# A mixture of experts whose product down is turned around: hidden units stationary, weights moving, and the shared expert as a ninth term of the same sum

## The chip, the cores and the metric

The kernel runs on one core of one Trainium2 chip, in f32 throughout. The metric is the time of one execution on the device, in microseconds. Engines are named as in the profile: PE is TensorE (PEld its weight loads), DVE is VectorE, ACT is ScalarE, POOL is GpSimd, SP is SyncE, which only issues DMAs here.

## The reference, cut to what matters

The input x has 8 batches of 1024 tokens with 128 features. Three layers follow one another, each behind a layer norm and each added to x: a feed-forward layer with weight 0.5, a causal attention with one head of 128, and the same feed-forward layer again. The feed-forward layer is a mixture of 16 experts with 64 hidden units each; a token uses its 4 best, and a shared expert with 64 hidden units is added for every token.

```python
scores = sigmoid(xt @ gate_w.T)
_, idx = top_k(scores + gate_b, 4)
w = take(scores, idx); w = w / w.sum() * 2.5
comb[t, idx] += w
...
for e in range(16):
    h = silu(xt @ gate_e.T) * (xt @ up_e.T)
    y = y + comb[:, e, None] * (h @ w2_e.T)
y = y + (silu(xt @ gate_s.T) * (xt @ up_s.T)) @ w2_s.T
x = x + 0.5 * y
```

## The kernel before

**Tiling.** All 16 experts are computed for all tokens, and comb is zero for those a token doesn't use. The unit of feed-forward work is a group of 512 tokens (W), four tiles of 128 (GT = 4). There are 8 batches x 2 groups x 2 feed-forward layers = 32 groups (NPER), done one after the other in a fixed order in which the second layer of one batch alternates with the first layer of the batch that is four further on. The 16 x 64 = 1024 hidden units are cut into NP = 8 blocks of 128, two experts each.

**One group.** The normed tokens lie transposed as hT, features by 512 tokens. For each block k, `up` (line 273) issues two matmuls of 128x512, gate (L271) and up (L284), with the weights stationary in the array; ScalarE takes silu of the one (L286), VectorE multiplies it with the other into hidT (L288), and `weigh` (L292, GpSimd) multiplies that by the token weights cb. Then `down` (L297) sums over the 8 blocks: the block of w2, wd, is stationary and hidT's 512 tokens move through it, so that y comes out transposed, features by tokens, in PSUM bank 0. `close` (L308, VectorE) adds the shared expert's part ys and leaves yT in SBUF. In the next group's time `add` has TensorE transpose yT in four pieces (L330), and VectorE adds half of it to x (L333); in the second layer a DMA stores it (L335). The last group does this in two halves (`add_last`, L318 to L321).

**The shared expert** is done for two groups at once (class Shared): `up` makes 128 columns of gate and up per group (L348), ScalarE and VectorE make h of it (L352, L353), with one group's 64 units on partitions 0 to 63 and the other's on 64 to 127. `down` multiplies the two halves by wsd on two row tiles of the array (L362, tile positions 0 and 64), and ScalarE copies the result to ys (L368).

**The route.** `turn` transposes the tokens (L174), route_a and route_b make the logits (L199, L208), top_a to top_c find the four best on VectorE and end with comb (L217 to L245), and `spread` transposes comb (L254), copies it, writes it to DRAM and reads it back broadcast over partitions as cb, all on SP's queue.

**Order.** Nothing is left to a scheduler. Every group's time p has 18 slots, U0 to U8 along its eight up steps and D0 to D8 along its eight down steps, and `at(p, slot, f)` puts work into a slot; its instructions go to each engine's queue in that order. Of group p's route, norm_a stands at (p-2, U5), norm_b at (p-2, D1), turn at (p-2, D4), route_a at D5, route_b and score at D7, top_a and top_b at D8, top_c at (p-1, U1) and spread at (p-1, U3). The attention's queries stand in between: a query's scores at U7, D2 or D4, its exp some slots later, its transpositions (L460, copied out at L464 by ScalarE or L466 by VectorE), and its product with v (L472, added to x at L476); those of one of the three queries fall on U3 of the next group. Shared.up stands at U0 and Shared.down at U2 of every second group; `add` of group p stands at (p+1, U3), and the statistics of the attention's norm for it at (p+1, U5) and (p+1, U7).

**PSUM.** There are eight banks of 128x512. Bank 0 holds y, banks 0 to 3 the up and gate products in turn, 2 to 5 the queries' scores, 4 and 5 also the shared expert. Everything else asks `other_bank`, which hands out the bank longest unused of 6, 7 and those of 1 to 5 that `hold` doesn't keep in this slot or a neighbouring one; banks 6 and 7 are handed out in any case. A bank that is still being read makes the next writer wait.

Of the kernel before, what the change touches and what calls it, by code (L numbers as in the profile page):

```python
# [9 lines left out]
F32 = mybir.dt.float32  # L10
AF = mybir.ActivationFunctionType
ALU = mybir.AluOpType
# [3 lines left out]
P = 128  # L16
# [10 lines left out]
def kernel(  # L27
# [14 lines left out]
    nc = tc.nc  # L42

    B, S, D = x.shape
    E = gate_w.shape[1]
    I = w_sh_down.shape[0]
    NT = S // P
    GT = 4
    NG = NT // GT
    W = GT * P  # L50
    EI = E * I
    NP = EI // P
# [3 lines left out]
    const = ctx.enter_context(tc.tile_pool(name="const", bufs=1))  # L56
# [3 lines left out]
    work = ctx.enter_context(tc.tile_pool(name="work", bufs=3))  # L60
# [8 lines left out]
    def bank(i, n=1):  # L69
        return psum[:, i * W : (i + n) * W]  # L70
# [5 lines left out]
    def other_bank():  # L76
        for n in by_age:
            free = not held[n] & {now[0] - 1, now[0], now[0] + 1} and now[0] >= 0
            if n > 5 or free:
                by_age.remove(n)  # L80
                by_age.append(n)
                return bank(n)

    def tiles_of(ap):
        return ap.rearrange("p (j q) -> p j q", q=P)

    ident = const.tile([P, P], F32, name="ident")
# [14 lines left out]
    xs, mvs = [None] * B, {}  # L102
# [27 lines left out]
    wd = const.tile([P, NP, D], F32, name="wd")  # L130
    nc.sync.dma_start(out=wd, in_=w_down.rearrange("(n p) d -> p n d", p=P))

    wsd = const.tile([P, D], F32, name="wsd")
    for n in range(2):
        nc.sync.dma_start(out=wsd[n * I : (n + 1) * I, :], in_=w_sh_down)
    wqkv = const.tile([P, 3, D], F32, name="wqkv")
    cs = const.tile([P, 2, S], F32, name="cs")

# [6 lines left out]
    def stats(key, b, tiles):  # L145

        if key not in mvs:
            mvs[key] = small.tile([P, NT, 2], F32, tag="mv", name=f"mv_{key}", bufs=16)
        for t in tiles:
            st = small.tile([P, 6], F32, tag="st", name=f"st_{key}_{t}")  # L150
            nc.vector.bn_stats(st, xs[b][:, t, :])
            nc.vector.bn_aggr(mvs[key][:, t, :], st)
# [26 lines left out]
    class Group:  # L179
# [111 lines left out]
            hid = self.hidT[:, k, :]  # L291
            nc.gpsimd.tensor_tensor(hid, hid, self.cb[:, k, :], ALU.mult)  # L292

        def down(self, k):
            if k == 0:
                self.y = bank(0)
            nc.tensor.matmul(  # L297
                self.y, wd[:, k, :], self.hidT[:, k, :], start=(k == 0), stop=(k == NP - 1)
            )

        def close(self):

            self.yT = work.tile([P, W], F32, tag="yT", name=f"yT_{self.nm}", bufs=2)
            halves = [slice(0, W)]
            if self.n == NPER - 1:
                halves = [slice(0, W // 2), slice(W // 2, W)]
            for c in halves:
                nc.vector.tensor_tensor(self.yT[:, c], self.y[:, c], self.ys[:, c], ALU.add)  # L308

        def add_last(self):  # L310

            H = GT // 2
            for n, queue in enumerate((nc.scalar, nc.sync)):
                yp = tiles_of(other_bank())[:, :H, :]
                t = self.g * GT + n * H
                for j in range(H):
                    k = n * H + j
                    nc.tensor.transpose(yp[:, j, :], self.yT[:, k * P : (k + 1) * P], ident)  # L318
                xg = xs[self.b][:, t : t + H, :]
                nc.vector.scalar_tensor_tensor(xg, yp, 0.5, xg, ALU.mult, ALU.add)  # L320
                queue.dma_start(  # L321
                    out=out[self.b].rearrange("(t p) d -> p t d", p=P)[:, t : t + H, :], in_=xg
                )

        def add(self):
            if self.n == NPER - 1:
                return self.add_last()
            yp = tiles_of(other_bank())
            for j in range(GT):
                nc.tensor.transpose(yp[:, j, :], self.yT[:, j * P : (j + 1) * P], ident)  # L330
            tiles = slice(self.g * GT, (self.g + 1) * GT)
            xg = xs[self.b][:, tiles, :]
            nc.vector.scalar_tensor_tensor(xg, yp, 0.5, xg, ALU.mult, ALU.add)  # L333
            if self.layer == 1:
                nc.sync.dma_start(  # L335
                    out=out[self.b].rearrange("(t p) d -> p t d", p=P)[:, tiles, :], in_=xg
                )

    class Shared:
# [5 lines left out]
        def up(self):  # L345
# [3 lines left out]
            for n, gr in enumerate(self.pair):  # L349
# [3 lines left out]
                nc.vector.tensor_tensor(  # L353
                    self.h[n * I : (n + 1) * I, :], s_ps[I:, :], ss[I:, :], ALU.mult
                )

        def down(self):
            H = W // 2
            for c in (slice(0, H), slice(H, W)):
                for n in range(2):  # L360
                    rows = slice(n * I, (n + 1) * I)
                    nc.tensor.matmul(  # L362
                        bank(5 - n)[:, c], wsd[rows, :], self.h[rows, c], start=True, stop=True,
                        tile_position=(n * I, 0),
                    )
            for n, gr in enumerate(self.pair):
                gr.ys = work.tile([P, W], F32, tag="ys", name=f"ys_{gr.nm}", bufs=2)
                nc.scalar.copy(gr.ys, bank(5 - n))  # L368

# [116 lines left out]
    NPER = NG * len(order)  # L488
# [7 lines left out]
    def at(p, slot, *fs):  # L496
        jobs.setdefault((p, slot), []).extend(fs)
# [3 lines left out]
    def when(p, slot):  # L501
        return p * len(slots) + slots.index(slot)

    def hold(banks, first, last):
        for n in banks:
            held[n] |= set(range(when(*first), when(*last) + 1))

    for p in range(NPER):
        hold((0,), (p, "U1"), (p, "D8"))
        hold((1,), (p, "U1"), (p, "U8"))  # L510
        hold((2, 3), (p, "U1"), (p, "D1"))
# [4 lines left out]
    queue = [(b, i) for b in range(B) for i in range(NT)]  # L516
# [47 lines left out]
    for p, gr in enumerate(groups):  # L564
        steps = (
            gr.norm_a, gr.norm_b, gr.turn, gr.route_a, gr.route_b, gr.score, gr.top_a, gr.top_b,
            gr.top_c, gr.spread,
        )
        if p == 1:
            steps = steps[1:]  # L570
            places = [(0, s) for s in ("U3", "U5", "U6", "U8", "D0", "D1", "D2", "D3", "D6")]
        else:
            places = [(p - 2, s) for s in ("U5", "D1", "D4", "D5", "D7", "D7", "D8", "D8")]
            places += [(p - 1, "U1"), (p - 1, "U3")]
        if p > 0:
            for f, place in zip(steps, places):
                at(*place, f)
        if gr.layer == 1:
            for t in range(gr.g * GT, (gr.g + 1) * GT):
                assert done[gr.b, t] < when(p - 2, "U5")  # L580

        if p % 2 == 0:
            pair = Shared(groups[p : p + 2])
            if p == 0:
                at(0, "D0", pair.up)
                at(0, "D3", pair.down)
                hold((4, 5), (0, "D0"), (0, "D4"))
            else:
                jobs[p, "U0"] = [pair.up] + jobs.get((p, "U0"), [])
                at(p, "U2", pair.down)  # L590
                hold((4, 5), (p, "U0"), (p, "U3"))

        at(p + 1, "U3", gr.add)
        if gr.layer == 0:
            t = gr.g * GT
            for s in ("U5", "U7"):
                at(p + 1, s, lambda b=gr.b, t=t: stats(f"a{b}", b, (t, t + 1)))
                t += 2


    for b in range(2, B):
        p = turn_of[0, b, 0]
# [13 lines left out]
    def run(p, slot):  # L616
        now[0] = when(p, slot)
        for f in jobs.pop((p, slot), []):
            f()

    gr = groups[0]
# [17 lines left out]
    for p, gr in enumerate(groups):  # L639
        run(p, "U0")  # L640
        for k in range(NP):
            gr.up(k)
            if p == 0 and k < 2:
                run(p, f"U{k + 1}")
                if k == 1:
                    gr.weigh(k)
            else:
                gr.weigh(k)
                run(p, f"U{k + 1}")
        for k in range(NP + 1):  # L650
            if k < NP:
                gr.down(k)
            if k == NP - 1:
                gr.close()
            run(p, f"D{k}")
    for p in (NPER, NPER + 1):
        for slot in slots:
# [73 lines left out]
```

## Time and profile before

| | |
|---|---|
| median of 3 runs | 994.64 us |
| lowest, highest | 994.27, 995.35 us |
| the profiled execution's own time | 994.21 us |
| its span in the profile | 992.3 us |
| TensorE's granted clock | 1.0 |
| product down (L297) | 512 matmuls, mean 599 ns |
| shared product down (L362) | 128 matmuls, mean 402 ns |
| transposition of y (L330) | 124 matmuls, mean 273 ns |
| ScalarE's copy to ys (L368) | 32, mean 589 ns |
| VectorE's sum yT (L308) and its addition to x (L333) | 33 at 673 ns and 31 at 681 ns |

The profile gives an instruction's line, engine, operation and tiles. A matmul of f32 appears as two records, a transposition as one, each with a load of its own on PEld. Matmuls are pipelined, so the records overlap and their mean duration is longer than the distance from one to the next. "Idle before" is the time in which an engine did nothing ahead of an instruction, with the releaser that ended it. The chain that ended last is followed back from the last instruction through what released each.

### The profile page before, as it was taken

How to read it: one execution, taken by the hardware profiler on the slowest of the kernel's cores; microseconds unless marked ns; L12 is line 12 of the kernel's file. 1: busy time of each engine (PE TensorE's matmuls, PEld its weight loads, DVE VectorE, ACT ScalarE, POOL GpSimd, SP SyncE). 2: the span in 40 equal slices, each digit the busy share in tenths (PEclk: the TensorE clock that was granted, in tenths of full speed). 3: DMA queues.
4: the chain of work that ended last, by engine and by line, in shares of the span. 5: the costliest groups of instructions: out<-in, count | busy, mean ns of one | idle time of the engine just before them, and what ended most of it. 6: DMA issues, size and time to landing. Idle time of an engine off the chain costs nothing.

```text
span 992.3 us, 11654 instructions
## 1 busy us (share of the span) xinstructions
PE 979.5 (99%) x3654; PEld 516.8 (52%) x3654; DVE 671.5 (68%) x2035; ACT 442.2 (45%) x798; POOL 450.5 (45%) x379
## 2 busy tenths in 40 slices
PE   8999999999999999999999999999999999999998
PEld 5444455555555555555555555555555555455543
DVE  5776787668666677766768756776667756665543
ACT  3444545444544445443544444544444444443331
POOL 2455556145633463344625455333643455423444
PEclk9999999999999999999999999999999999999999
DMA  6655443043413532145303453044421344134440
GB/s 165 163 118 105 87 87 87 2 107 87 87 28 70 119 86 48 40 97 118 87 18 70 97 118 81 8 84 97 98 59 42 73 97 94 33 68 97 97 97 21
DMA packets 56909, 80.25 MB, mean 81 GB/s; under 512 B 3600, under 2 KB 23440, under 8 KB 56720
## 3 DMA queue, kind: packets, MB, share of 16 engines
q1 hardware_dynamic: 55568, 78.26, 35.4%
q10 hardware_dynamic: 1280, 1.26, 0.4%
q8 instruction: 28, 0.46, 0.2%
q14 instruction: 33, 0.27, 0.1%
HBM read 74.27 MB, written 5.24 MB: 80 GB/s over the span
## 4 chain that ended last, share of the span: by engine, by line
PE 93%; DVE 3%; ACT 1%; DMA 1%; issue 0%; POOL 0%; SPq 0%; POOLq 0%; DVEq 0%
PE psum L297 22%; PE psum L271 21%; PE psum L284 21%; PE psum L472 6%; PE psum L433 6%; PE psum L460 3%; PE psum L348 3%; PE psum L400 3%; PE psum L174 2%; PE psum L362 2%; PE psum L414 1%; PE psum L199 1%; PE psum L330 1%; DMA cb<-cd 1%; PE psum L254 1%; PE psum L141 1%
## 5 line engine op out<-in xcount | busy, mean ns | idle before, releaser
L292 POOL TENSOR_TENSOR hidT<-hidT,cb 128x512 f32<-128x512 f32 x256 | 323.0, 1269 | 502.5 <-DVE hidT L288 464.4
L271 PE MATMUL psum<-hT,wg 128*128 128x512 f32 x512 | 263.7, 597 | 0.5 <-ACT prT L464 0.5
L284 PE MATMUL psum<-hT,wu 128*128 128x512 f32 x512 | 261.9, 593 | 0.6 <-DVE hidT L288 0.5
L297 PE MATMUL psum<-hidT,wd 128*128 128x512 f32 x512 | 247.1, 599 | 0.0
L288 DVE TENSOR_TENSOR hidT<-psum,sg 128x512 f32<-128x512 f32 x256 | 175.4, 687 | 104.1 <-PE psum L284 95.9
L286 ACT ACTIVATE sg<-psum 128x512 f32<-128x512 f32 x256 | 151.8, 597 | 196.9 <-PE psum L271 185.8
L284 PEld LDWEIGHTS psum<-hT,wu 128*128 128x128 f32 x512 | 96.9, 190 | 124.1 <-issue 95.7
L297 PEld LDWEIGHTS psum<-hidT,wd 128*128 128x128 f32 x512 | 89.9, 190 | 80.3 <-issue 73.2
L271 PEld LDWEIGHTS psum<-hT,wg 128*128 128x128 f32 x512 | 88.1, 191 | 67.3 <-issue 58.3
L472 PEld LDWEIGHTS psum<-v,prT 128*128 128x128 f32 x576 | 74.4, 192 | 30.6 <-issue 28.5
L472 PE MATMUL psum<-v,prT 128*128 128x128 f32 x576 | 74.6, 275 | 0.0
L433 PE MATMUL psum<-k,q 128*128 128x512 f32 (+2 forms) x192 | 72.4, 486 | 0.0
L464 ACT COPY prT<-psum 128x512 f32<-128x512 f32 (+2 forms) x64 | 32.3, 505 | 86.2 <-PE psum L460 86.1
L165 DVE TENSOR_SCALAR xn_f<-x,mv_f,rs_f 128x128 f32<-128x128 f32 x128 | 68.8, 597 | 2.5 <-POOL rs_f L158 2.4
L308 DVE TENSOR_TENSOR yT<-psum,ys 128x512 f32<-128x512 f32 (+1 forms) x33 | 22.1, 673 | 58.0 <-PE psum L297 57.6
L433 PEld LDWEIGHTS psum<-k,q 128*128 128x128 f32 x192 | 36.5, 190 | 45.9 <-issue 44.5
L460 PEld LDWEIGHTS psum<-ident,pr 128*128 128x128 f32 x288 | 36.0, 141 | 30.0 <-issue 29.6
L439 DVE TENSOR_REDUCE top<-psum 128x1 f32<-128x128 f32 (+3 forms) x64 | 48.5, 758 | 2.2
L444 ACT ACTIVATE pr<-psum,top 128x128 f32<-128x128 f32 (+3 forms) x64 | 47.7, 745 | 0.3
L437 DVE TENSOR_TENSOR psum<-psum,causal 128x128 f32<-128x128 f32 x64 | 19.0, 296 | 41.3 <-PE psum L433 40.8
L460 PE MATMUL psum<-ident,pr 128*128 128x128 f32 x288 | 46.5, 273 | 0.0
L175 ACT COPY hT<-psum 128x512 f32<-128x512 f32 x32 | 18.7, 585 | 47.7 <-PE psum L174 47.7
(86 smaller groups left out, 1023.7 us busy)
## 6 DMA issues: line engine op xcount, KB each, us to landing
cb<-cd SPq DMA_DIRECT2D x124, 512.0 KB, 8.0
x<-in_x SPq DMA_DIRECT2D x16, 256.0 KB, 10.7
out_x<-x SPq DMA_DIRECT2D x15, 256.0 KB, 2.4
cb<-cd SPq DMA_DIRECT2D x8, 256.0 KB, 6.1
cd<-cT SPq DMA_DIRECT2D x32, 32.0 KB, 2.0
cs<-in_rope SPq DMA_DIRECT2D x1, 1024.0 KB, 9.3
wg<-in_w_gate ACTq DMA_DIRECT2D x2, 256.0 KB, 7.3
wu<-in_w_up ACTq DMA_DIRECT2D x2, 256.0 KB, 6.9
```

Of the source, the lines that this page charges most:

```text
L165: nc.vector.tensor_scalar(xn[:, j, :], xs[b][:, t, :], mvs[key][:, t, 0:1], rstd[:, j : j + 1], ALU.subtract, ALU.mult,)
L271: nc.tensor.matmul(bank(2 * (k % 2) + 1), wg[:, units], self.hT, start=True, stop=True)
L284: nc.tensor.matmul(u_ps, wu[:, units], self.hT, start=True, stop=True)
L286: nc.scalar.activation(sg, g_ps, AF.Silu)
L288: nc.vector.tensor_tensor(hid, u_ps, sg, ALU.mult)
L292: nc.gpsimd.tensor_tensor(hid, hid, self.cb[:, k, :], ALU.mult)
L297: nc.tensor.matmul(self.y, wd[:, k, :], self.hidT[:, k, :], start=(k == 0), stop=(k == NP - 1))
L433: nc.tensor.matmul(s[:, c:e], h.q[:, i * P : width], h.k[:, c:e], start=True, stop=True)
L439: nc.vector.tensor_reduce(top, s[:, :width], AX.X, ALU.max)
L444: nc.scalar.activation(self.pr[:, : self.width], self.s[:, : self.width], AF.Exp, bias=self.top, scale=SCALE, accum_out=self.h.rl[:, self. ...
L460: nc.tensor.transpose(tp[:, j, :], self.pr[:, (k + j) * P : (k + j + 1) * P], ident)
L472: nc.tensor.matmul(o, self.prT[:, j, :], self.h.v[:, j, :], start=(j == 0), stop=(j == i))
```

## The change

The product down is turned around. For each block k and each of the group's four token tiles j, the 128x128 piece of hidT is loaded as the stationary operand, and the block of wd (128x128) moves. y comes out as tokens by features, in four 128-column slices of bank 0, which is how x lies. The shared expert becomes a ninth term of this sum: `down_shared` multiplies h's 128 rows (both groups' units) by a wsd that holds w2_s in the 64 rows of its own group and zeros in the others, ahead of the eight blocks (in group 0 at D3, between them). The flag `start`, which makes a matmul overwrite what its bank holds, is set on the first matmul of a group in the bank alone.

`close`, `add_last`, Shared.down, yT, ys and the transpositions are gone. `add` reads bank 0 directly, right behind the last block, where `close` stood, and the store of a second-layer group is issued there too. Banks 4 and 5 are held for the shared expert at U0 and U1 only, not up to U3. The last group does the whole sum for its first two tiles in bank 0, adds and stores them from ScalarE's queue, and then does the other two in bank 1 with SP's queue.

```diff
-    wsd = const.tile([P, D], F32, name="wsd")
+    wsd = const.tile([P, 2, D], F32, name="wsd")
     for n in range(2):
-        nc.sync.dma_start(out=wsd[n * I : (n + 1) * I, :], in_=w_sh_down)
+        rows = slice(n * I, (n + 1) * I)
+        nc.vector.memset(wsd[rows, 1 - n, :], 0.0)
+        nc.sync.dma_start(out=wsd[rows, n, :], in_=w_sh_down)
...
-        def down(self, k):
-            if k == 0:
-                self.y = bank(0)
-            nc.tensor.matmul(
-                self.y, wd[:, k, :], self.hidT[:, k, :], start=(k == 0), stop=(k == NP - 1)
-            )
...
+        def y_of(self, j):
+            return bank(0 if self.n < NPER - 1 or j < GT // 2 else 1)[:, j * P : (j + 1) * P]
+
+        def down(self, k, tiles=range(GT)):
+
+            for j in tiles:
+                nc.tensor.matmul(
+                    self.y_of(j), self.hidT[:, k, j * P : (j + 1) * P], wd[:, k, :],
+                    start=(k == 0 and self.n == 0 and j == tiles[0]),
+                    stop=(k == NP - 1 and j == tiles[-1]),
+                )
+
+        def down_shared(self, tiles=range(GT)):
+
+            for j in tiles:
+                nc.tensor.matmul(
+                    self.y_of(j), self.sh[:, j * P : (j + 1) * P], wsd[:, self.n % 2, :],
+                    start=(self.n > 0 and j == tiles[0]), stop=False,
+                )
+
+        def add(self, tiles=range(GT), queue=nc.sync):
+            n = 0 if tiles[0] == 0 else 1
+            y = tiles_of(bank(n))[:, tiles[0] : tiles[-1] + 1, :]
+            ts = slice(self.g * GT + tiles[0], self.g * GT + tiles[-1] + 1)
+            xg = xs[self.b][:, ts, :]
+            nc.vector.scalar_tensor_tensor(xg, y, 0.5, xg, ALU.mult, ALU.add)
+            if self.layer == 1:
                 queue.dma_start(
...
             if p == 0:
                 at(0, "D0", pair.up)
-                at(0, "D3", pair.down)
-                hold((4, 5), (0, "D0"), (0, "D4"))
+                at(0, "D3", gr.down_shared)
+                hold((4, 5), (0, "D0"), (0, "D1"))
             else:
                 jobs[p, "U0"] = [pair.up] + jobs.get((p, "U0"), [])
-                at(p, "U2", pair.down)
-                hold((4, 5), (p, "U0"), (p, "U3"))
-
-        at(p + 1, "U3", gr.add)
+                hold((4, 5), (p, "U0"), (p, "U1"))
...
+        if p == NPER - 1:
+
+            for tiles, queue in ((range(GT // 2), nc.scalar), (range(GT // 2, GT), nc.sync)):
+                gr.down_shared(tiles)
+                for k in range(NP):
+                    gr.down(k, tiles)
+                gr.add(tiles, queue)
+            break
+        if p > 0:
+            gr.down_shared()
         for k in range(NP + 1):
             if k < NP:
                 gr.down(k)
             if k == NP - 1:
-                gr.close()
+                gr.add()
             run(p, f"D{k}")
```

More of the change, by code (lines that the diff above doesn't have):

```diff
@@ L292, in weigh @@
             nc.gpsimd.tensor_tensor(hid, hid, self.cb[:, k, :], ALU.mult)
-        def down(self, k):
-            if k == 0:
-                self.y = bank(0)
-            nc.tensor.matmul(
-                self.y, wd[:, k, :], self.hidT[:, k, :], start=(k == 0), stop=(k == NP - 1)
-            )
[L301 to L320, printed above, removed]
-                queue.dma_start(
-                    out=out[self.b].rearrange("(t p) d -> p t d", p=P)[:, t : t + H, :], in_=xg
-                )
@@ L325, in add @@
[L325 to L336, printed above, removed]
+        def y_of(self, j):
+            return bank(0 if self.n < NPER - 1 or j < GT // 2 else 1)[:, j * P : (j + 1) * P]
@@ new lines, in add @@
+        def add(self, tiles=range(GT), queue=nc.sync):
[5 more added lines that the diff above has]
+            if self.layer == 1:
+                queue.dma_start(
+                    out=out[self.b].rearrange("(t p) d -> p t d", p=P)[:, ts, :], in_=xg
@@ L355, in up @@
                 )
[L357 to L368, printed above, removed]
+                gr.sh = self.h
     class Heads:
@@ L506, in hold @@
             held[n] |= set(range(when(*first), when(*last) + 1))
+    hold((1,), (NPER - 1, "D0"), (NPER - 1, "D8"))
     for p in range(NPER):
```

## The prediction

> **What bounds the kernel now.** I read the page's busy line first, then the chain that ended last, then the groups of instructions by form, and then the chain in order of time in stretches of 12 to 30 us.
>
> ```profile
> PE 979.5 (99%) x3654; PEld 516.8 (52%) x3654; DVE 671.5 (68%) x2035; ACT 442.2 (45%) x798; POOL 450.5 (45%) x379
> PE 93%; DVE 3%; ACT 1%; DMA 1%; issue 0%; POOL 0%; SPq 0%; POOLq 0%; DVEq 0%
> ```
>
> TensorE is the bound, nearly without a hole. So ScalarE's copy of ys (L368) and VectorE's yT (L308), which the change drops, free engines that have 55% and 32% to spare. What counts is TensorE's own time, and what TensorE waits for at a few places. The groups by form (count after the x; busy us, mean ns) give the counts:
>
> ```profile
> L297 PE MATMUL psum<-hidT,wd 128*128 128x512 f32 x512 | 247.1, 599 | 0.0
> ...
> L472 PE MATMUL psum<-v,prT 128*128 128x128 f32 x576 | 74.6, 275 | 0.0
> ...
> L330 PE MATMUL psum<-ident,yT 128*128 128x128 f32 x124 | 18.6, 273 | 0.0
> L362 PE MATMUL psum<-sh,wsd 64*128 64x256 f32 x128 | 18.2, 402 | 0.0
> ```
>
> 256 calls of the product down are 512 records: each f32 product runs as two passes, and a transposition as one. Mean durations overlap, so the price of a pass is the distance from one matmul's end to the next. The chain in order of time (start, us, what) shows it:
>
> ```profile
> 510.63 1.78 PE psum L472 x16
> 512.42 1.06 PE psum L362 x8
> 513.48 1.05 PE psum L271 x2
> 514.54 0.86 PE psum L284 x2
> 515.39 0.44 PE psum L330 x4
> ...
> 522.81 0.89 PE psum L414 x8
> ...
> 527.36 2.58 PE psum L297 x6
> ```
>
> A pass with 512 moving columns costs 0.43 us (2.58/6), one with 128 costs 0.111 (1.78/16, 0.89/8), not a quarter of 0.43, which would be 0.107. Over the whole trace, end to end and with waits left out, I get 429.2 ns and 111.4 ns (L472, mean of 576), and 109.3 for a transposition's pass (L330, mean of 124). The L271 behind L362 takes 1.05 where the others take 0.86.
>
> **What the Trainium skill says.** "TensorE: Matmul & The Clock Gate", section "LDWEIGHTS (loading the stationary operand)": a load takes the columns divided by 1.2 in ns, 107 for 128 columns, and the section on weight-path modes says that the fast load is not for FP32. The trace agrees: a 128-column pass with a load of its own cannot go below about that, and measures 111.4, while behind a 429 ns pass the load is hidden (PEld is busy 190 ns and then idle about 240). "TensorEngine Tiling (Array Packing)", section "Key Properties": changing the tiling mode drains TensorE. The trace agrees: 0.20 us more at the first L362 and 0.20 us more behind the last.
>
> **The change part by part,** against the profiled execution (994.21 us, span 992.3).
>
> *Down, by tokens.* 256 steps go from two wide passes (858 ns) to eight narrow ones with a load each. L414 is this shape exactly: four slices of one bank, the weights moving, a new stationary block each time. 2048 x 111.4 = 228.2 against 512 x 429.2 = 219.8: **+8.4**.
>
> *Shared expert as ninth term.* 32 groups x 8 passes x 111.4 ns = **+28.5**. It is not cheaper for its 64 useful rows, as wsd is filled with zeros to 128. Gone is L362: it ran two row tiles side by side, 17.0 us end to end over the 16 pairs, and with 16 x 0.198 for the drains behind it **-20.2**.
>
> *Transpositions of y.* 124 passes at 109.3: **-13.6**. The last group's four are in the tail below. TensorE's work so far: +3.1.
>
> *Waits at the spread (L254, slot U3).* Here TensorE loses time today. L254 transposes comb, and these are its waits by source:
>
> ```profile
>   ACT prT L464: 6.3, 18
>   DVE comb L245: 6.1, 7
> ```
>
> Taking every L254's end-to-end distance above 110 ns, start-up apart: 4.1 us in 11 groups is for a bank that ScalarE still copies prT out of. L254 is the third transposition in slot U3 there, behind L460 and L330, and other_bank comes back to L460's bank. Without L330 it is the second, and banks 4 and 5 come free two slots earlier, so this goes: **-4.1**. Another 1.6 us in 4 groups is for comb, at the end of a chain on VectorE that starts when down ends:
>
> ```profile
> 218.92 0.04 DVE yT L308
> ...
> 223.47 1.27 DVE sel L239
> ...
> 225.22 0.28 DVE comb L245
> 225.51 0.04 issue
> 225.55 0.30 PE psum L254
> ```
>
> That chain takes 6.6 us from yT to comb. In the changed kernel add stands in yT's place (0.68 us at L333 against 0.69 at L308), so comb comes no earlier, but TensorE reaches L254 sooner: by 0.44 us without L330, and in every second group by another 1.25 without L362 (1.06 and the drain). I took L254's start less the end of comb for every group and subtracted: of the 15 groups without L362 after the first two, the four that wait now wait 0.44 more each, 3.35 in all, the nearest of the others keeps 0.12; of the 15 with it, those with slacks of 1.16, 1.82, 1.65, 1.66, 1.82 and 1.16 (some of it wait for the bank already) come out 0.59, 0.25, 0.31, 0.31, 0.25 and 0.59 us late, 2.3 in all; the others had 2.6 or more and keep at least 0.4. So 5.6 us of waits for comb stand where 1.6 stood: **+4.0**. What L330 and L362 covered comes back here, and cancels the bank's 4.1.
>
> *Start-up.* At 58.18 us TensorE waits 1.0 us for xn_f (L174, slot D4), whose chain hangs on slot U5; eight passes of the shared term and four or five longer down steps now lie between, about 1.05 us, and fill it: -1.0. A like wait of 0.4 us at 82.9: -0.4. At 34.0 the work ahead of the wait gets 0.2 shorter: +0.2. **-1.2.**
>
> *The end.* From the chain, at the end:
>
> ```profile
> 980.75 6.88 PE psum L297 x16
> 987.63 0.02 issue
> 987.65 0.43 DVE yT L308
> 988.09 0.04 issue
> 988.13 0.45 PE psum L318 x2
> 988.59 0.02 issue
> 988.61 0.81 DVE x L320 x2
> ```
>
> From TensorE's end to the last sum are 1.79 us. In the changed kernel one half is added and sent while TensorE works on the other, and behind TensorE's end only one addition of 256 columns (0.41, half of L320's two) and the 0.02 remain: **-1.36**. The last weigh ends at 982.9 and the first half needs it near 984.3, so no wait takes its place.
>
> *Edits at nothing.* ScalarE's 32 ys copies (17.2 us) and VectorE's 33 yT (22.1) go, under TensorE. Two memsets stand at VectorE's start, where it waits for x (2.9 us, L151); uncovered they'd cost less than 0.3. SP's queue: the store of a layer-1 group is issued at D7 and not at U3 of the next; behind it come a load of x (D8) and the cb copies, all with more time than before. The add at D7 holds VectorE's queue until down ends, as yT did, with the route's chain behind it. TensorE's program grows by 1536 loads and as many matmuls, 42%. Its instructions come in fetches of 16 KB (28 now, one per 256 instructions, about 1.2 us each); 256 instructions last 14 us at the narrow pace and no matmul waits at a fetch today: nothing, and if that cover failed, some 40 fetches of 1.2 us.
>
> *Two things the trace doesn't show.* Eight-pass blocks with a semaphore at their head, 288 of them: from nothing (L414's first pass, 110 ns) to 51 ns each (the semaphore instruction in PE's queue), 14.7 us; I take nothing, as the weights are ready long before. The narrow pace: from 109.3 (-4.8 us) to 112 (+1.4); the low end needs a load as short as the transposition's (141 ns busy against 192), which hidT's is not, so I take 111.4.
>
> **The sum:** +8.4 +28.5 -20.2 -13.6 -4.1 +4.0 -1.2 -1.4 = +0.4, within its own rounding +0.4 to +0.6. That gives 994.8 for an execution like the profiled one; the median of the three runs, 994.64, is 0.43 above that, so **995.2 us**. Its own range is 993.7 to 996.8, as the start-up and each of the two waits may be off by about 1.
>
> **Rivals.**
> *Faster: the comb chain comes earlier.* In some groups yT starts out of a backlog on VectorE (near 412 us right behind L151, without idle). The D slots get 1.16 us longer, which lets that backlog drain, and U3's addition is gone. If comb came half a us earlier against TensorE, six of the ten waits would lose 0.5 and four vanish: 4.1 us, **991.1**. Against it: near 219 and in most groups VectorE had been idle for us before yT.
> *Slower: the bank's wait stays.* If other_bank still gave L254 a bank that is being read in those 11 groups, each would wait its 0.37 and the 0.44 that L330 covered: 4.1 + 4.8 = 8.9, **1004.1**. It decides from 0.13 us in each of the 11 groups on. For it: banks 6 and 7 are handed out whatever holds them, and the turn order shifts. Against it: banks 4 and 5 are the ones longest unused.
> *Slower: the reversal doesn't run at L414's pace* because each block waits at its head: 14.7 us, **1009.9**. Against it: L472 and L414 have such heads and show none.
>
> **How the numbers follow.** The measurement of this kernel can tell about 0.2%, 2 us, from no change. Forecast 0.63, faster rival 0.17, bank 0.13, heads 0.07. The range 990.9 to 997.9 takes in the forecast and the faster rival, and leaves out the two slower ones. Of the forecast's 0.63, 0.56 lies within 0.2%, 0.06 above and 0.01 below; so faster 0.18, same 0.56, slower 0.26.
>
> **What would show it.** Right: down with 2048 records and the shared term with 256, 0.89 us for eight in the chain; L330 and L362 gone; L254's waits now for comb and not for prT, over 5 us; about 3.3 us from TensorE's end to the end of the span. Wrong: eight passes at 0.95 or more, L254 waiting on ScalarE or on x (L476), or fewer waits for comb than today.

## The result and the profile after

The changed kernel takes 996.61 us (median of 19 runs, 995.80 to 998.16) against 994.75 (median of 19, 994.01 to 996.24). The ratio is 1.0018, with a 95% interval of 1.0011 to 1.0025: 1.9 us slower, just within the 0.2% that the prediction called no change, though with so many runs the interval excludes a ratio of 1. The profiled execution took 997.42 us with a span of 995.6. It lies 0.81 above its median, while the one of before lies 0.54 below its own, so of the 3.2 us between the two spans 1.35 is the choice of execution.

TensorE still has hardly a hole, and its weight loads went from 52% to 66%:

```profile
PE 980.9 (99%) x5190; PEld 657.0 (66%) x5190; DVE 652.3 (66%) x2004; ACT 425.1 (43%) x766; POOL 450.3 (45%) x379
PE 90%; DVE 7%; ACT 1%; issue 1%; POOL 0%; ACTq 0%; POOLq 0%; DVEq 0%
```

The second line is the chain's share by engine. VectorE's part of it grew from 3% to 7%, TensorE's fell from 93% to 90%. The groups by form (idle time before them at the end) show the new records: 2048 and 256, and no L362 and L330 any more. The last line is the transposition of comb, L254 before.

```profile
L302 PE MATMUL psum<-wd,hidT 128*128 128x128 f32 x2048 | 255.9, 276 | 0.0
...
L311 PE MATMUL psum<-wsd,sh 128*128 128x128 f32 x256 | 33.9, 275 | 0.0
...
L256 PE MATMUL psum<-ident,comb 128*64 128x128 f32 x32 | 9.0, 282 | 5.0 <-DVE comb L247 4.6
```

The chain in order of time, near 514 and 529 us, has the up steps of slots U2 and U3 without anything between them but the query's product and comb, and the new sum at its pace, 0.89 for eight passes:

```profile
513.88 1.78 PE psum L448 x16
515.66 0.86 PE psum L273 x2
516.52 0.86 PE psum L286 x2
517.38 0.11 PE psum L256
...
528.91 0.89 PE psum L311 x8
529.80 2.68 PE psum L302 x24
```

Before, 1.06 and a drain stood behind the query's product, and 0.44 ahead of comb. In other groups a wait for VectorE fills that place. This is the group whose chain was shown before:

```profile
220.18 0.04 DVE x L321
...
224.73 1.27 DVE sel L241
...
226.49 0.29 DVE comb L247
226.78 0.04 issue
226.82 0.30 PE psum L256
```

From the addition that closes the group to comb are 6.6 us, as before, and TensorE arrives earlier: it waits 0.71 us here where it waited 0.27. Who waited for whom at L256 has turned over too, from ScalarE's copy to comb (total us, times; the idle time of the weight loads is counted too, so that this is more than the 5.5 us that TensorE's matmuls lose behind the first two groups):

```profile
  DVE comb L247: 18.1, 23
```

And the end of the span:

```profile
988.29 0.45 PE psum L311 x4
988.74 3.59 PE psum L302 x32
992.32 0.02 issue
992.35 0.43 DVE x L321
```

3.3 us lie between TensorE's end and the end of the span, 4.7 before.

Laid out by line, from one matmul's end to the next (TensorE's time with its waits):

| us | predicted | measured |
|---|---|---|
| product down | +8.4 | 226.0 to 234.5: +8.5 |
| shared expert | +28.5 - 20.2 | 28.5 - 17.0, and 15 drains of 0.2 (the 16th lies in the line above): +8.5 |
| transpositions of y | -13.6 | -13.55 |
| waits at L254 or L256 behind the first two groups | -4.1 + 4.0 | 5.7 to 5.5: -0.2 |
| other waits of the start-up | -1.2 | +0.5 |
| the end | -1.36 | -1.44 |
| a wait not foreseen, a gate matmul at 475 us | 0 | +0.77 |

These terms sum to +3.1, of 3.24 between the spans. The +0.5 of the start-up is -0.2 at the transpositions of normed tokens (L174, now L176), +0.3 at gate and up matmuls between 92 and 97 us, and +0.4 in the first 38 passes of all (L141, now L143: the identity times itself), of which 20 and not 16 took 213 ns instead of 112. This last is not the change's: in the fourteen profiles of this document it is 11 to 26 of them.

### The profile page after: what moved, and what is told of

Same layout as the page of the kernel before. It is cut to its first block, busy times and chain, and to the rows that moved or that the text cites. A ratio compares the mean times of both kernels' runs of the same rounds, so it can differ in the third digit from the quotient of the medians.

```text
span 995.6 us, 14631 instructions
## 1 busy us (share of the span) xinstructions
PE 980.9 (99%) x5190; PEld 657.0 (66%) x5190; DVE 652.3 (66%) x2004; ACT 425.1 (43%) x766; POOL 450.3 (45%) x379
## 3 DMA queue, kind: packets, MB, share of 16 engines
q10 hardware_dynamic: 1280, 1.26, 0.4%
## 4 chain that ended last, share of the span: by engine, by line
PE 90%; DVE 7%; ACT 1%; issue 1%; POOL 0%; ACTq 0%; POOLq 0%; DVEq 0%
PE psum L302 23%; PE psum L273 20%; PE psum L286 19%; PE psum L409 6%; PE psum L448 6%; PE psum L436 3%; PE psum L311 3%; PE psum L376 3%; PE psum L176 2%; PE psum L336 2%; PE psum L390 1%; DVE sel L241 1%; PE psum L201 1%; DVE hidT L290 1%; PE psum L143 1%
## 5 line engine op out<-in xcount | busy, mean ns | idle before, releaser
L294 POOL TENSOR_TENSOR hidT<-hidT,cb 128x512 f32<-128x512 f32 x256 | 322.8, 1269 | 505.1 <-DVE hidT L290 316.7
L302 PE MATMUL psum<-wd,hidT 128*128 128x128 f32 x2048 | 255.9, 276 | 0.0
L302 PEld LDWEIGHTS psum<-wd,hidT 128*128 128x128 f32 x2048 | 242.3, 192 | 12.3 <-issue 10.3
L290 DVE TENSOR_TENSOR hidT<-psum,sg 128x512 f32<-128x512 f32 x256 | 175.3, 687 | 92.4 <-PE psum L286 86.1
L448 PEld LDWEIGHTS psum<-v,prT 128*128 128x128 f32 x576 | 72.4, 192 | 18.2 <-issue 16.3
L321 DVE SCALAR_TENSOR_TENSOR x<-psum,x 128x512 f32<-128x512 f32 (+1 forms) x33 | 22.2, 674 | 64.7 <-PE psum L302 64.6
L409 PEld LDWEIGHTS psum<-k,q 128*128 128x128 f32 x192 | 33.6, 191 | 27.7 <-issue 26.8
L311 PEld LDWEIGHTS psum<-wsd,sh 128*128 128x128 f32 x256 | 33.6, 192 | 14.8 <-issue 11.2
## 6 DMA issues: line engine op xcount, KB each, us to landing
x<-in_x SPq DMA_DIRECT2D x16, 256.0 KB, 10.9
```

What stands on the lines that cost most here:

```text
L290: nc.vector.tensor_tensor(hid, u_ps, sg, ALU.mult)
L302: nc.tensor.matmul(self.y_of(j), self.hidT[:, k, j * P : (j + 1) * P], wd[:, k, :], start=(k == 0 and self.n == 0 and j == tiles[0]), stop ...
L311: nc.tensor.matmul(self.y_of(j), self.sh[:, j * P : (j + 1) * P], wsd[:, self.n % 2, :], start=(self.n > 0 and j == tiles[0]), stop=False,)
L409: nc.tensor.matmul(s[:, c:e], h.q[:, i * P : width], h.k[:, c:e], start=True, stop=True)
L448: nc.tensor.matmul(o, self.prT[:, j, :], self.h.v[:, j, :], start=(j == 0), stop=(j == i))
```

## Experiments

**The route's last step moved behind one more up step, in both kernels.** In each, this line is the only edit:

```diff
-            places += [(p - 1, "U1"), (p - 1, "U3")]
+            places += [(p - 1, "U1"), (p - 1, "U4")]
```

In the changed kernel:

> The changed kernel with one edit: the transposition of comb (spread) stands in slot U4 and not in U3, behind one more pair of up matmuls (1.72 us). Theory: what the change takes off TensorE between the route's chain on VectorE and this transposition came back as waits for comb, 5.5 us of them behind the start-up, none over 1.04 us, so all are covered: 996.6 - 5.5 = 991.1 us, and no wait over 0.1 us at L256 except in the start-up. Rival: VectorE's chain is the bound in these slots and TensorE waits for it elsewhere (at an up or gate matmul, for a bank): within 1 us of 996.6.

Measured: 993.86 us, ratio to the kernel before 0.9987 (0.9980 to 0.9994). Runs of different chips are best compared by such ratios, and from 1.0018 this is 3.1 us less, somewhat over half of what my theory gave. L256's waits behind the first group are gone altogether, but in six of the same groups an up matmul now waits, 0.70 us at 99 and 0.44 to 0.49 at 70, 225, 419, 543 and 950:

```profile
222.31 1.27 DVE sel L241
...
224.07 0.03 DVE comb L247
224.10 0.11 issue
224.21 0.69 DVE hidT L290
224.91 0.04 issue
224.95 1.12 PE psum L286 x2
226.07 0.11 PE psum L256
```

The second product of hidT (L290 at 224.21) stands behind the route's chain in VectorE's queue, and the up matmul writes into the bank that it has to read first. So theory and rival were each half right: the waits are of the route, and moving its reader alone lets part of them, 3.0 us, appear one bank further on.

In the kernel before:

> The kernel before with the same one edit: spread in slot U4 and not in U3. Theory: both kinds of wait at L254 go, 1.6 us for comb and 4.1 us for a bank that ScalarE still copies out of, since 1.72 us of TensorE's work come between: 994.75 - 5.7 = 989.0 us, which would leave the change 2.1 us slower with either place of spread. Rival: the waits move to other places: within 1 us of 994.75. A third reading, that other_bank's turn then gives a bank that VectorE reads late: the 1.6 us alone goes, 993.1.

Measured: 990.48 us, ratio 0.9955 (0.9942 to 0.9967), 4.5 us less, of the 5.7. No L254 behind the first group waits, neither for comb nor for the bank; one up matmul at 101 us takes 0.6 over. The kernel before thus carried over 4 us of waits that one line takes out. It shows no such wait later, since L330 and L362 still stand ahead of that matmul: the 0.49 of the changed kernel at 225 and 543 us, less L330's 0.44, leaves 0.05, and 0.05 is what stands there. With this place of spread in both, the changed kernel is 3.2 us slower by the ratios, where 2.1 was expected.

**The cover taken away alone.** In the kernel before, the transpositions of y, which stood ahead of L254, come one slot later:

```diff
-        at(p + 1, "U3", gr.add)
+        at(p + 1, "U4", gr.add)
```

> The kernel before with one edit: add (the four transpositions of y and the addition to x) stands in slot U4 and not in U3, so that spread follows a query's transpositions directly. This does to L254's bank and to its cover what taking L330 away does, without the rest of the change. Theory: the bank's wait of 4.1 us in 11 groups goes, as L254 is then the second and not the third to ask for a bank in U3; the four groups that wait for comb wait 0.44 us longer each, 1.75: 994.75 - 2.3 = 992.4 us. Rival: the wait on the copy of prT has nothing to do with the order in which banks are handed out and stays or grows by the 0.44 us that L330 covered, 4.8 us: 999 to 1001.

Measured: 992.87 us, ratio 0.9979 (0.9971 to 0.9986): 2.3 us less than 995.14 on the same chip, as the theory said. The wait for the copy of prT no longer appears at L254, and comb is what it waits for; at the four groups near 100, 226, 420 and 543 us the wait is now 1.26, 0.72, 0.68 and 0.72, each 0.44 more. These lines of L254's waits (total us, times, the loads' idle time counted too) and the chain show it:

```profile
  DVE comb L245: 13.8, 15
```

```profile
225.92 0.28 DVE comb L245
226.20 0.05 issue
226.25 0.30 PE psum L254
```

So the two halves of this step, a bank's wait that goes and a cover that is missed, are each shown, in different groups of one run and without the rest of the change.

**The shared expert's product left out, in both.** In the changed kernel:

```diff
-                    start=(k == 0 and self.n == 0 and j == tiles[0]),
+                    start=(k == 0 and j == tiles[0]),
...
-                at(0, "D3", gr.down_shared)
...
-                gr.down_shared(tiles)
...
-        if p > 0:
-            gr.down_shared()
```

> The changed kernel without the shared expert's product down: down_shared is left out, its h is still made, and y lacks that term; the first of the eight blocks starts the sum. Theory: the ninth term is TensorE's time one for one, 32 x 8 passes at 111.4 ns = 28.5 us, hidden by nothing but some 0.9 us of a wait in the start-up: 996.6 - 28.5 = 968.1, up to 969. Rival: part of it stands in waits that the D slots have anyway, so that less is saved: 975 or more.

Measured: 970.23 us, ratio 0.9749 (0.9734 to 0.9764), 26.8 us less than the changed kernel by the ratios. That is 1.2 us over the 969 that the theory allowed. The records are 28.5 us fewer, and the waits behind the start-up are the same to 0.1 us; the rest came back in the start-up, where TensorE now waits 2.05 us for xn_f at 34 us instead of 0.86. So the ninth term is paid one for one wherever TensorE is the bound.

In the kernel before, the four L362 of `Shared.down` are left out:

```diff
-            H = W // 2
-            for c in (slice(0, H), slice(H, W)):
-                for n in range(2):
-                    rows = slice(n * I, (n + 1) * I)
-                    nc.tensor.matmul(
-                        bank(5 - n)[:, c], wsd[rows, :], self.h[rows, c], start=True, stop=True,
-                        tile_position=(n * I, 0),
-                    )
```

> The kernel before without the shared expert's product down: L362 is left out (its copy to ys and the sum yT stay and carry whatever the banks hold, so y is not the reference's). Theory: 17.0 us of L362 and 3.0 us of drains behind it go, and 0.3 us of waits for comb come where L362 was the cover: 994.9 - 19.7 = 975.2. The changed kernel without its ninth term took 970.2, so the reversal alone would be worth 5.0 us, and the ninth term would lose it. Rival: L362 is cheaper than that since its drains overlap with waits: 978 or more.

Measured: 980.66 us, ratio 0.9857 (0.9842 to 0.9872), 14.2 us less and not 19.7. The records and the drains are gone, 20.0 us, so my theory of the work stands, but not of the waits: 1.3 us more in the start-up, 1.1 less at L254, and 4.9 us at L330 in five groups, of which none was expected:

```profile
127.66 0.68 DVE hidT L288
128.34 0.27 DVE x L468
128.61 0.04 issue
128.66 0.66 PE psum L330 x4
129.31 0.11 PE psum L254
```

L330 had been given the bank out of which VectorE adds a query's result to x (L468 here, L476 before), which is done behind the chain and the second product. With L362 ahead of it this was early enough. So this pair doesn't give the price of the reversal alone, as I had meant it to: 970.2 against 980.7 contains these waits. It does show L362 as the cover of a wait, with its price.

**What limits a narrow pass.**

```diff
-                    self.y_of(j), self.hidT[:, k, j * P : (j + 1) * P], wd[:, k, :],
+                    self.y_of(j)[:, : P // 2], self.hidT[:, k, j * P : (j + 1) * P],
+                    wd[:, k, : P // 2],
...
-                    self.y_of(j), self.sh[:, j * P : (j + 1) * P], wsd[:, self.n % 2, :],
+                    self.y_of(j)[:, : P // 2], self.sh[:, j * P : (j + 1) * P],
+                    wsd[:, self.n % 2, : P // 2],
```

> The changed kernel with half of the moving columns in the reversed products: 64 of 128 of wd and of wsd move, so y's upper 64 features are left out; loads and count are as before. Theory: a pass is bound by its own load of 128 columns, so 2304 passes keep 107 to 111 ns and the time falls by no more than 10 us: 987 to 997. Rival: the pass is bound by the columns that move, and the load is hidden: about 56 ns a pass, 2304 x 55 = 127 us less, 870.

Measured: 995.01 us, ratio 1.0001 (0.9992 to 1.0010). Half of these products' multiplications are gone, and by the ratios 1.7 us of the time. Eight passes take 0.84 us instead of 0.89:

```profile
528.37 0.84 PE psum L312 x8
529.21 2.68 PE psum L302 x24
```

End to end, passes inside a block keep 112 and 111 ns, and only 117 that follow other work, mostly a wide matmul under which their load was hidden, take 55 to 60. So at 64 moving columns the load is the limit, and a stationary block of 128 columns costs its load. At 128 moving columns the columns alone cost about as much: in `after`, the 93 narrow passes behind a wide matmul, whose load is done before that matmul ends (at 52.36 us under one that ends at 52.76), take 109 to 111 ns, 109.6 in the mean, against 111.6 for the others. There the load of its own adds 2 ns. The median hides part of what was saved: in the profile, passes from 36.97 to 43.80 us run at half pace, about 3.1 us longer in all, at a granted clock of 0.5 (part of which comes back, as no wait is left at 58 us); the mean clock of eight of the ten runs is 0.995 or 0.996, as in the profiled one, and the two others, at 992.01 and 993.28 us, are the fastest.

**The rest of the route's waits.** `top_c` was cut in two behind sel's product (the new `top_d`), and the places were, for both kernels:

```diff
-            places += [(p - 1, "U1"), (p - 1, "U3")]
+            places += [(p - 1, "U2"), (p - 1, "U3"), (p - 1, "U4")]
```

> The changed kernel with the route's last VectorE work moved too: sel and its product at U2, behind the second product of hidT, the rest of it at U3, and spread at U4. With spread alone at U4 the waits for comb went, but 3.0 us of them came back in the same groups at an up matmul (0.44 to 0.70 us each), whose bank VectorE had not read yet, as that product stands behind the route's chain in its queue. Theory: with the product ahead of the chain these go as well, and all 5.5 us are saved: 996.6 - 5.5 = 991.1 us. Rival: VectorE is behind its work as a whole in these slots, and the wait moves one matmul on: 993.9, as with spread at U4 alone.

Measured: 1008.50 us, ratio 1.0138 (1.0124 to 1.0151), the wrong way by 12 us, and neither reading had it. L260 (the transposition of comb here) waits 0.7 to 1.7 us in 14 groups: I had moved comb later by more of TensorE's work than its reader. With the second half behind the third product of hidT, comb is ready 2 us after TensorE's third up step, and the fourth takes 1.7:

```profile
228.13 0.68 DVE hidT L294
...
229.18 1.11 DVE comb L251
230.29 0.04 issue
230.33 0.30 PE psum L260
```

> The kernel before with the same edit (sel at U2, the rest at U3, spread at U4). With spread at U4 alone it showed 1.0 us of waits behind the start-up, none of them for comb. Theory: the route no longer bounds there, so nothing more is to be had: 990.5 us within 0.7. Rival: the start-up, where one up matmul waits 0.6 us for VectorE, gains as well: 989.9.

Measured: 995.98 us, ratio 1.0009 (1.0001 to 1.0018), against 990.48 with spread at U4 alone. It's the same mistake, smaller, since L330 stands ahead of the reader.

With `top_c` whole at U2 and spread at U5:

```diff
-            places += [(p - 1, "U1"), (p - 1, "U3")]
+            places += [(p - 1, "U2"), (p - 1, "U5")]
```

> The changed kernel with the route's last VectorE part (top_c) whole at U2, behind the second product of hidT, and spread at U5. With the same part split and spread at U4 the waits for comb grew to 1.1 to 1.7 us in 14 groups, since its second half then stood only 1.7 us of TensorE's work ahead of its reader. Theory: what the route costs TensorE is the distance in TensorE's work between comb's place and its reader, against what stands ahead of comb on VectorE; with three up steps between nothing is left: 991.2 us, 2.5 to 3 us under spread at U4 alone. Rival: VectorE is behind as a whole, and the third product of hidT, now behind the chain, makes the fifth up matmul wait: 993 to 995.

Measured: 990.84 us, ratio 0.9957 (0.9945 to 0.9970). Of the route's waits 0.22 us is left, in one group, and the chain's shares by engine are

```profile
PE 98%; ACT 1%; DVE 1%; issue 0%; POOL 0%; POOLq 0%
```

> The kernel before with the same edit (top_c at U2, spread at U5). Theory: with the route out of the way in both, what is left between this and the changed kernel with the same edit is TensorE's own work (8.5 + 28.5 - 20.0 - 13.6 = +3.4 us) less the end (1.4): 2.0 us apart, so 989 to 990 us here. Rival: as above for VectorE, 992 or more.

Measured: 990.29 us, ratio 0.9949 (0.9937 to 0.9961). Here the two kernels stand side by side without the route: 0.55 us apart where I had 2.0, with intervals too wide to tell these from each other. By their spans it is 1.4 us (989.0 against 987.6): 3.4 us of work, less 1.4 at the end, less 1.05 of start-up waits, and 0.3 of others come to 1.25 of it. Both have a wait of 0.78 us at the gate matmul near 470 us, which the kernel before had not had.

**The start-up.** The third batch's x is loaded earlier:

```diff
-            at(p - 4, "D8", lambda b=b, g=g: load_x(b, g))
+            at(p - 4, "D8" if b > 2 else "U8", lambda b=b, g=g: load_x(b, g))
```

> The changed kernel with the loads of the third batch's x issued at U8 and not at D8 of the first group, so that they are done before the copies of group 1's token weights (cb) run. Theory of the start-up wait at 58 to 60 us (1.55 us in the profile): its chain hangs on cb's landing, which shares the DMA engines with these 0.5 MB; cb lands 1 us or more earlier, the wait at L176 goes, and up to 1.5 us are saved: 995.1 to 996.1. Rival, as in the prediction: the chain hangs on slot U5, and nothing changes: 996.6.

Measured: 996.52 us, ratio 1.0013 (1.0007 to 1.0020), which can't be told from the changed kernel's 1.0018. In its profile GpSimd starts on group 1's weights at 47.07 instead of 48.46, and the wait at 58 to 60 us is 0.44 instead of 1.55. But `after_spread_u4`, with the loads where they were, shows 46.97 and 0.24. So the wait goes with GpSimd's start, and this differs by 1.5 us between profiles. The theory's cause doesn't hold either: the copy of cb that GpSimd waits for (its second) landed 6.79 us after its issue with the edit, 6.62 in `after_spread_u4`, and 7.70 in `after`, so the loads beside it don't make it late.

**The bank of the first gate matmul.** To `after_route_u5`, behind the line that holds bank 1 in the up slots:

```diff
+        if p < NPER - 1:
+            hold((1,), (p, "D7"), (p + 1, "U0"))
```

> after_route_u5 with bank 1, into which each group's first gate matmul writes, kept from other_bank at D7, D8 and the next U0. Three waits of that matmul are left there, 0.77 us at 470, 0.73 at 851 and 1.67 at 92, the last two also in one form or another in the kernel before. Theory: they stand there because other_bank handed out bank 1 in D7 or D8 and its reader on ScalarE comes late; which group meets it is an accident of the turn order, which the change shifted (0.77 us at 475 is new with it). They go: 1.5 us and part of the 1.67, so 988 to 989.4 against 990.84, below the kernel before with the same route (990.29). Rival: other banks then carry the same wait, 990.8.

Measured: 989.79 us, ratio 0.9942 (0.9928 to 0.9956). The waits at 470 and 851 us are gone, 1.5 us in the profile, and the 1.67 at 92 became 0.43 and 0.71 at two up matmuls that VectorE holds. The medians are 1.05 us apart. It lies 5.3 us under the kernel before on the same chip, and can't be told from `before_route_u5`.

## Why the prediction was right, and where it was not

The forecast was 995.2 us and no change that can be told; measured were 996.61 and 1.9 us more. It lies in the range, and 0.2 us inside the upper end of the forecast's own. Between the two profiles, for which the terms were worked out, it is 3.24 us where +0.4 was forecast, so the forecast owes some of its closeness to the medians, which leave out the 1.35 of the two executions.

**Right: TensorE's work.** All four terms came within 0.2 us, and their sum within 0.4 (8.5 + 8.5 - 13.55 = +3.45, for +3.1). The pace of 111.4 ns, taken from L472 and L414, held for 2304 new passes (L311 has a mean of 111.4), and blocks with semaphores at their head paid nothing. That a load sets a floor, which the prediction had argued from a page and from PEld's idle time only, `after_half_moving` shows for 64 moving columns; at 128 the columns alone cost 109.6 of the 111.4, so there the number came out right though the load is hardly its reason.

**Right: what the bank's wait gives is taken back for comb.** The ten groups named as late are the ten that wait, with 5.5 us in all where 5.6 was worked out, and `before_add_u4` shows both halves one by one. The rival "the bank's wait stays" fell: no L256 behind the start-up waits for ScalarE. So did "comb comes earlier": the chain from the closing sum to comb is 6.6 us in both kernels in the group shown, and in the other groups, with up to 10.0 us, the two kernels lie within 0.2 of each other.

**Right: the end,** 1.44 for 1.36, and the edits at nothing.

**Wrong in this profile, though not in others: the start-up, -1.2.** The step was "whose chain hangs on slot U5 ... about 1.05 us, and fill it". The chain of xn_f at 58 us does not hang on U5. It goes back over GpSimd's queue, which starts on group 1's weights at 47.22 us before and 48.46 after, 10.0 and 10.9 behind that group's transposition of comb. Before, the trace puts this start down to the landing of cb, and after to VectorE, but the landings that it records settle it: cb's second copy landed at 47.06 and 48.30, each time 0.16 ahead of GpSimd's start, and took 6.83 and 7.70 us from its issue. With that the wait was 1.55 us instead of none, and the longer D slots gained nothing in this profile.

The late copy is of this execution. In four other profiles of the changed kernel, with its products and its loads as they were (`after_spread_u4`, `after_route_late`, `after_route_u5`, `after_route_u5_bank1`) the copy takes 6.62 to 6.71 us and the wait is 0.24 to 0.36, against 0.80 to 1.29 in the five of the kernel before that keep its shared product. So the D slots do fill most of this wait, and between the two route_u5 profiles the start-up gives 1.05 of the foreseen 1.2. How much of it the median holds stays open. At 34 us the waits grew by 0.24, as foreseen; those at 82.9 went, 0.8 us where 0.4 was counted.

**Not foreseen: other_bank's turn.** It was weighed for L254 alone, while the one order serves every caller. With one call less per group, the group near 475 us got bank 1 for the attention's transposed tokens, which ScalarE copies out (hT_a, L177), and the next gate matmul writes there: 0.77 us. It is an accident of the turn: in `before_route_u5`, which moves two steps of the route only, the same bank falls to the same tokens, with the same wait. Around 92 to 97 us three waits of 0.42, 0.16 and 0.75 turned into one of 1.67, for the logits of a route that stand in bank 1 until ScalarE has read them (L215). `after_route_u5_bank1` takes away the wait at 475 and its fellow at 851, which the kernel before has too. The prediction also took each wait as if it ended there; `after_spread_u4` shows that behind comb's stands another of VectorE's, worth half of it.

Against the forecast's +0.55 the medians differ by +1.86. The 1.3 between them are of the size of what was not in the sum, 0.77 at 475 us, 0.3 near 94 us and 0.3 more of TensorE's work, but the start-up differs by as much from one execution to the next, and the runs don't settle how much of each the median holds.

## What to carry to other kernels

Price a turned product by its loads: at 128 moving columns load and columns cost about alike, at 64 the load's 111 ns stay, so the turn saves nothing by itself and must pay with what it makes unnecessary (here 13.6 us of transpositions and 1.4 at the end, against 8.5 for the product itself), and a term with 64 useful rows, filled up to 128 with zeros, cost 111.4 ns a pass like a full one. Work that is taken off a bound engine may have been the cover of another engine's chain: take the slack of each reader from the trace, one instance at a time, and look at who is next in that other queue. Where banks are handed out in turn, one call less shifts them for every later caller. And when such slacks decide, moving the reader can be worth more than the change: one line gave 4.5 us in the kernel before.

## What the runs showed of the hardware that I had not expected

- TensorE's granted clock can fall behind a short wait. In `after_no_shared`, behind the 2.05 us in which TensorE waited at 34 us, eight narrow passes took 1.92 us (35.26 to 37.18) where they take 1.06 elsewhere; the clock granted is 0.5 from 35.08 to 38.50. In `after_half_moving` it is 0.5 from 36.52 to 43.35, behind a wait of only 1.27 us there. In `before_no_shared` it stays at 1.0 behind a wait of 1.83. So the length of the wait alone doesn't decide it, and what does stays open.
- A short VectorE operation on SBUF can take as long as GpSimd's work beside it. In `after`, sel's product (L241) takes 0.22 to 0.23 us in the three groups in which GpSimd stands still, and 1.25 to 1.32 in the other 29, in each of which it ends 0.08 or 0.09 behind GpSimd's multiplication (L294). In `after_route_late` it is comb (L251), 0.27 to 0.28 in the same three and 1.03 to 1.12 in the 29, ending 0.12 to 0.15 behind. So the route's 6.6 us hold about one such second in 29 of 32 groups.
